# Three whole-tile additions of a two-layer graph kernel issued as accumulating transfers

## Chip, cores and metric

The kernel runs on one core of a Trainium2 chip. The metric is the device time of one execution in microseconds (us); lower is better. The engines are named as in the profile: PE is TensorE's matrix multiply and PEld its weight load, DVE is VectorE, ACT is ScalarE, POOL is GpSimd, SP is SyncE, which here only issues transfers.

## What is computed

The input is x, 16 batches of 1024 rows of 256 numbers, and an integer matrix adj of 0s and 1s, 16 x 1024 x 1024. Two graph layers follow one another, each wrapped in a residual and a layer norm:

```python
# layer 0: 4 heads of 64
h   = einsum('bnd,hde->bhne', x, W)
w   = leaky_relu(mask of edges * (e_src + e_dst));  no edge: -1e9
out = relu(softmax(w) @ h + bias) + h
out = layernorm_per_head(out) * ln_gamma + ln_beta
x   = layernorm(x + out)
# layer 1: 8 heads of 32
normed = layernorm(x) * gamma1 + beta1
out = softmax(where(adj > 0, normed @ normed.T / sqrt(32), -inf)) @ normed
x   = x + out                               # x before this line is x_in below
y   = layernorm(x) * gamma2 + beta2
mlp = gelu(y @ W1 + b1) @ W2 + b2          # 256 -> 1024 -> 256
x   = layernorm(x_in + (x + mlp))          # x_in: input of layer 1
```

The three additions that the change touches are: ln_beta to x (the "beta" of layer 0, so that one later addition brings both into the sum), the attention's output to the residual of layer 1, and b2 to that residual.

## The kernel before

All matrix work is in float32. A batch of 1024 rows is worked in two halves of 512 rows; a half lies in a tile of 128 partitions x 4 blocks x 256 numbers (128 x 1024, 512 KB). Two generators write the program: layer0 (line 955) runs over the batches and does preparation and attention of layer 0, and layer1 (line 973) follows one batch behind with attention and MLP of layer 1. A loop at the end of fast_path (from about line 1019) takes turns between them, so that PE always has the work of two batches to choose from.

The order on PE, ACT, DVE and POOL is the order in which the program is written; the loop chooses it from a model of time. The class Pace (line 90) passes every instruction on to its engine and books a start and an end for it by a table of costs; `enter` (line 151) books a transfer as landing 4 us after it may start. Work off the main line is written as chains: generators that `begin` (line 431) puts on a list with an engine and the tiles they need, and that `advance` (line 446) runs a step further once the model says that these are ready. `complete` (line 458) writes the rest of a chain at once. A step's place in an engine's queue is thus fixed by the model; on the chip an engine only waits for semaphores. SP's order is set by another scheduler, which moves a load up to where its buffer is free.

The tiles live in rings (class Ring, line 66); the ring `one` has one buffer of a name, `two` has two, and so on. xl and o0 are in `one`, x1 in `three`, layer 1's weights p in `eight`. PSUM has four buffers ps for the logits and first-layer products, two acc, two po.

The places that the change and the prediction touch:

- **Layer 0, after the attention (after0, line 638).** It runs for a pair of heads, so twice a half (hd = 1 and hd = 3), on the tile hb, called o there. DVE subtracts the mean per head, ACT squares (into oT), DVE sums (v0s), POOL takes the power -1/2 (tile r; `power`, line 347), DVE multiplies by gamma and then by r. With hd = 3 the tile xl is taken and x loaded into it by SP (line 657), DVE adds ln_beta to it (line 668), and DVE adds xl to hb (line 674). From there the norms that lead to layer 1's input (sq, nT, v) and to its residual x1 follow.
- **Layer 0's attention (attention0, line 567)** needs DVE for its weights (p<-cb,dinv,mask) and PE for acc<-v,p; preparation (prepare, line 484) puts acc<-w0e,xT on PE, small copies and `rows` on ACT, z<-acc,bias and v<-z,v on DVE.
- **Layer 1's attention (attention1, line 722).** A step: four logits matmuls on PE into the four ps, four exponentials on ACT (p<-ps), two mask products on DVE (p<-p,mask), and, three steps later, PE's products (po<-p,v, po<-p,unit, po<-v,p). PE can write the logits of the next step only when ACT has read the ps buffers. A half takes 16 steps; the tile o0 (o<-po,ranges) gathers its heads.
- **The residual of layer 1 (finish1, line 840),** once a half: DVE adds x1 to o (o<-o,x), takes statistics, writes v1s; POOL takes the power (r<-v1s); DVE adds o to x1 (x<-x,o, line 852) and computes t; ACT normalises o **in place** with four activations (o<-o,t,r; scale_shift, line 362); PE transposes o (acc or ps<-ident,o) and ACT copies it to yT. So o is read by the addition of line 852 and then overwritten by ACT.
- **The bias (add_bias2, line 861),** a chain of its own that half_done (line 986) begins, due 24 us of model time later: x1 += b2 on DVE. Here b2_r holds b2 - beta1.
- **The MLP (mlp, line 872).** PE forms ps<-yT,w_sb, ACT the Gelu (hid<-ps,b_sb), PE po<-w_sb,hid. `second` (line 889) completes the bias chain before it starts; last_norm (line 931) adds x1 to po on DVE (z<-po,x), norms it with a power on POOL and four small steps, and SP stores it.

The first half's finish1 falls in the middle of layer 1's attention, the second half's at the start of the MLP. POOL also issues the loads of adj (tile ak, line 476), which turn int32 into bfloat16 on the way.

Of the kernel before, what the change touches and what calls it, by code (L numbers as in the profile page):

```python
# [31 lines left out]
F32 = mybir.dt.float32  # L32
# [4 lines left out]
OP = mybir.AluOpType  # L37
PSUM = bass.MemoryType.PSUM

P = 128  # L40
# [49 lines left out]
class Pace:  # L90
# [60 lines left out]
    def enter(self, engine, op, args, kwargs):  # L151
        aps = [a for a in (*args, *kwargs.values()) if isinstance(a, bass.AP)]
        out, ins = aps[0].tensor.name, [a.tensor.name for a in aps[1:]]
        if op == "dma_start":
            start = max(self.now(), self.through(out))
            self.written[out] = start + self.LATENCY["sync"]
            return
        start = max(
            [self.free[engine], self.read.get(out, 0.0)] + [self.written.get(i, 0.0) for i in ins if i != out]
        )  # L160
        cost = self.cost(engine, op, aps, args[2] if len(args) > 2 else None)
        if engine == "tensor":
            if start > self.free[engine] + 1.5:
                self.slow = start + 3.0
            if start < self.slow:
                cost *= 2.0
        end = self.free[engine] = start + cost
        self.written[out] = max(self.written.get(out, 0.0), end + self.LATENCY[engine])
        if "accum_out" in kwargs:
            out = kwargs["accum_out"].tensor.name  # L170
            self.written[out] = max(self.written.get(out, 0.0), end + self.LATENCY[engine])
        for i in ins:
            self.read[i] = max(self.read.get(i, 0.0), end)
# [3 lines left out]
def fast_path(  # L177
# [24 lines left out]
    nc = Pace(tc.nc)  # L202
# [112 lines left out]
    def at_time(t):  # L315
        return lambda: t
# [141 lines left out]
    def complete(chain):  # L458

        for item in list(chains):  # L460
            if item[0] is chain:
                while item in chains:
                    run(item)


    def load_x(t, b, k, count):
        nc.sync.dma_start(t, x[b, k * P : (k + count) * P, :].rearrange("(g p) d -> p g d", p=P))
# [170 lines left out]
    def after0(b, n, hd, o):  # L638


        for first in range(hd + 1):
            complete(residuals[b, n, first])
        rowwise = [P, BPH, D]
        heads = slice((hd - PAIR + 1) * HO, (hd + 1) * HO)
        oh = o[:, :, heads].rearrange("p g (h e) -> p g h e", e=HO)
        per_head = [P, BPH, PAIR, HO]
        s = small.tile([P, BPH, PAIR], F32, name="s0")
        nc.vector.tensor_reduce(s, oh, axis=mybir.AxisListType.X, op=OP.add)
        nc.vector.scalar_tensor_tensor(
            oh, s[:, :, :, None].to_broadcast(per_head), -1.0 / HO, oh, op0=OP.mult, op1=OP.add  # L650
        )
        yield "scalar", o
        sq = two.tile([P, BPH, PAIR * HO], F32, name="oT1")
        nc.scalar.activation(sq, o[:, :, heads], AF.Square)
        if hd == H0 - 1:
            xl = one.tile(rowwise, F32, name="xl")
            load_x(xl, b, n * BPH, BPH)
        yield "vector", sq
        v = small.tile([P, BPH, PAIR], F32, name="v0s")
        nc.vector.tensor_reduce(  # L660
            v, sq.rearrange("p g (h e) -> p g h e", e=HO), axis=mybir.AxisListType.X, op=OP.add
        )
        nc.vector.tensor_scalar(v, v, 1.0 / HO, EPS_HEAD, op0=OP.mult, op1=OP.add)
        r = power(v.rearrange("p g e -> p (g e)"), BPH * PAIR, "r0").rearrange("p (g e) -> p g e", e=PAIR)
        pair = o[:, :, heads]
        nc.vector.tensor_mul(pair, pair, lng0_r[:, None, heads].to_broadcast([P, BPH, PAIR * HO]))
        if hd == H0 - 1:
            nc.vector.tensor_add(xl, xl, lnb0_r[:, None, :].to_broadcast(rowwise))
        yield "vector", r
        nc.vector.tensor_mul(oh, oh, r[:, :, :, None].to_broadcast(per_head))  # L670
        if hd < H0 - 1:
            return
        complete(norms[b, n, PAIR - 1])
        nc.vector.tensor_add(o, o, xl)
        yield "vector", o
        mv = small.tile([P, BPH, 2], F32, name="mv0")
        for g in range(BPH):
            statistics(o[:, g, :], mv[:, g, :])

        v2 = small.tile([P, 2, BPH], F32, name="v2")
        nc.vector.tensor_scalar(v2[:, 0, :], mv[:, :, 1], 1.0 + EPS, EPS * EPS, op0=OP.mult, op1=OP.add)
        r2 = power(v2[:, 0, :], BPH, "r2")
        nc.vector.tensor_scalar(v2[:, 1, :], mv[:, :, 1], EPS, None, op0=OP.add)
        r3 = power(v2[:, 1, :], BPH, "r3")
        yield "vector", r2
        t = minus_mean(mv[:, :, 0], r2, BPH)
        yield "scalar", t
        normed = one.tile(rowwise, F32, name="sq")  # L690
        scale_shift(normed, o, t, r2, BPH)
        yield "tensor", normed, side_ready
        nT = two.tile([P, DC, HALF], F32, name="nT")
        for g in range(0, BPH, GB):
            transpose_rows(nT[:, :, g * P : (g + GB) * P], normed[:, g : g + GB, :], g1_c, be1_c)
            yield "tensor", normed, side_ready
        yield "vector", normed
        v1 = two.tile([P, BPH, H1, HD + 1], F32, name="v1")
        nc.vector.memset(v1[:, :, :, HD], 1.0)
        for g in range(BPH):  # L700
            nc.vector.tensor_mul(
                v1[:, g, :, 0:HD],
                normed[:, g, :].rearrange("p (h e) -> p h e", e=HD),
                g1_r.rearrange("p (h e) -> p h e", e=HD),
            )
        handed[b, n] = [None, v1, nT]
        yield "vector", r3

        ratio = small.tile([P, BPH], F32, name="ratio")
        nc.vector.tensor_mul(ratio, v2[:, 0, :], r2)  # L710
        nc.vector.tensor_mul(ratio, ratio, r3)
        yield "vector", ratio, at_time(nc.now() + 12.0)

        x1 = three.tile(rowwise, F32, name="x1")
        for g in range(BPH):
            nc.vector.scalar_tensor_tensor(
                x1[:, g, :], normed[:, g, :], ratio[:, g : g + 1], be1_r, op0=OP.mult, op1=OP.add
            )
        handed[b, n][0] = x1
# [120 lines left out]
    def finish1(o, x1, yT, heads):  # L840


        complete(heads)
        rowwise = [P, BPH, D]
        nc.vector.tensor_add(o, o, x1)
        mv = small.tile([P, BPH, 2], F32, name="mv1")
        for g in range(BPH):
            statistics(o[:, g, :], mv[:, g, :])
        v = small.tile([P, BPH], F32, name="v1s")
        nc.vector.tensor_scalar(v, mv[:, :, 1], EPS, None, op0=OP.add)  # L850
        r = power(v, BPH, "r1")
        nc.vector.tensor_add(x1, x1, o)
        yield "vector", r
        t = minus_mean(mv[:, :, 0], r, BPH)
        yield "scalar", t
        scale_shift(o, o, t, r, BPH)
        for g in range(0, BPH, GB):
            yield "tensor", o, side_ready
            transpose_rows(yT[:, :, g * P : (g + GB) * P], o[:, g : g + GB, :])

    def add_bias2(x1):
        nc.vector.tensor_add(x1, x1, b2_r[:, None, :].to_broadcast([P, BPH, D]))
        yield from ()

    def in_range(values):
# [78 lines left out]


    handed = {}
    norms, residuals = {}, {}

    def finish_norms(b, n):
        for chain in [c for at, c in norms.items() if at[:2] == (b, n)]:  # L950
# [22 lines left out]
    def layer1():  # L973
        for b in range(B):
            place[1][:] = b, 0.0
            seen, rinv1, mask = handed.pop(b)

            def half(n):
                if (b, n) not in handed:
                    finish_norms(b, n)  # L980
                return handed[b, n]

            yT = [two.tile([P, DC, HALF], F32, name="yT") for _ in range(NH)]
            halves = {}

            def half_done(n, o, heads):
                finish_norms(b, n)
                x1 = handed[b, n][0]
                chain = finish1(o, x1, yT[n], heads)
                bias = add_bias2(x1)  # L990
                halves[n] = x1, yT[n], chain, bias
                begin(chain, "vector", done(heads), o)
                begin(bias, "vector", at_time(nc.now() + 24.0), x1)

            yield from attention1(half, mask, rinv1, half_done)
            complete(weights_of_later)
            yield from mlp(b, halves)
            in_range(seen)
# [490 lines left out]
```

## Time and profile before

| | us |
|---|---|
| three runs | 3454.31, 3445.69, 3454.04 |
| median | 3454.04 |
| span of the profiled execution, first to last instruction | 3453.7 |
| the profiled execution's own time | not listed apart from its span |
| PE busy | 3312.8 (96%) |
| DVE busy | 2981.3 (86%) |
| ACT busy | 1935.6 (56%) |
| POOL busy | 418.6 (12%) |
| mean granted clock of PE | 0.980 |

How to read the profile. A group line names the source line (L61 for all, since one helper records every instruction, so tiles tell the groups apart), the engine, the operation, out<-in by the program's tile names without their numbers, and the shape; then busy us and mean ns of one, and after the second bar the idle time of the engine just before these instructions with what ended it. A timeline line begins with the start and the length in us; in square brackets stands idle time before it. In a line of the waits the numbers are us in total, how many times, and the longest. In the table of stretches every engine has its busy time in that stretch. "issue" means that the engine waited for nothing that the profile shows. The chain of waits is followed back from the last instruction, at each step to what released it. A queue line of transfers gives packets, MB and the share of 16 transfer engines that they took; an issue line gives KB each and the median us from issue to landing. Several waits ending together are put down to the last one.

### The profile page before, as it was taken

The page shows a single profiled execution, that of the slowest core. Times are in us where ns is not written, and L with a number is a line of the kernel's source. Part 1 is how long each engine was busy: PE and PEld are TensorE (multiplying, and loading weights), DVE is VectorE, ACT ScalarE, POOL GpSimd, SP SyncE. Part 2 cuts the span into 40 slices and gives each one's busy share as a digit, 9 for nine tenths or more (in the row PEclk, how much of TensorE's full clock was granted, in tenths as well). Part 3 has the DMA queues.
Part 4 walks back from the last instruction along what each step waited for, and adds up shares of the span by engine and source line. Part 5 has one row for each costly group of instructions (what it writes and reads, how often), then busy time and mean ns, then how long its engine had stood idle before and what let it go on. Part 6 is the DMA issues. An engine that isn't in the chain of part 4 may idle for free.

```text
span 3453.7 us, 141035 instructions
## 1 busy us (share of the span) xinstructions
PE 3312.8 (96%) x64161; PEld 2252.1 (65%) x64161; DVE 2981.3 (86%) x5262; ACT 1935.6 (56%) x4192; POOL 418.6 (12%) x424
## 2 busy tenths in 40 slices
PE   5899999999999999999999999999999999999998
PEld 4558576675856758576585766757667585775846
DVE  5898898988979898898988989889898898989883
ACT  2563846547375573746637466473654737556373
POOL 1102011010110101101020110101101011010200
PEclk9899999999999999999999999999999999999999
DMA  5211202011020111202112020120201102010000
GB/s 135 51 22 40 44 27 57 15 44 40 28 59 21 42 34 34 56 19 59 22 38 46 24 57 19 41 43 26 59 15 46 38 28 62 18 44 23 23 6 15
DMA packets 95728, 131.30 MB, mean 38 GB/s; under 512 B 10385, under 2 KB 61585, under 8 KB 95121
## 3 DMA queue, kind: packets, MB, share of 16 engines
q1 hardware_dynamic: 75104, 87.58, 8.2%
q0 software_dynamic: 18432, 33.56, 6.6%
q8 instruction: 504, 8.26, 1.0%
q10 hardware_dynamic: 1584, 1.05, 0.1%
q14 instruction: 104, 0.84, 0.1%
HBM read 138.68 MB, written 17.04 MB: 45 GB/s over the span
## 4 chain that ended last, share of the span: by engine, by line
PE 72%; DVE 20%; ACT 5%; issue 2%; DMA 1%; POOL 0%; SPq 0%; POOLq 0%; ACTq 0%; DVEq 0%
PE po L61 28%; PE ps L61 24%; PE acc L61 20%; DVE p L61 15%; ACT p L61 2%; DVE o L61 1%; DVE x L61 1%; ACT sq L61 1%; DVE st L61 1%; DVE z L61 1%; ACT mask L61 1%; ACT hb L61 1%; DVE v L61 0%; ACT z L61 0%; DVE hb L61 0%
## 5 line engine op out<-in xcount | busy, mean ns | idle before, releaser
L61 ACT ACTIVATE p<-ps 128x512 f32<-128x512 f32 x2006 | 1042.2, 616 | 384.1 <-PE ps L61 341.5
L61 DVE TENSOR_TENSOR p<-p,mask 128x1024 f32<-128x1024 f32 x1024 | 1186.6, 1217 | 6.8 <-ACT p L61 6.8
L61 DVE SCALAR_TENSOR_TENSOR p<-cb,dinv,mask 128x512 f32<-128x512 f32 x1024 | 711.0, 744 | 0.1
L61 ACT ACTIVATE hid<-ps,b_sb 128x256 f32<-128x256 f32 x512 | 242.0, 473 | 795.0 <-PE ps L61 794.7
L61 PE MATMUL ps<-nT 32*128 32x512 f32 x4012 | 676.3, 655 | 0.0
L61 PEld LDWEIGHTS po<-v,p 128*32 128x32 f32 x32768 | 396.1, 110 | 333.2 <-issue 288.5
L61 PE MATMUL acc<-v,p 128*64 128x65 f32 x16384 | 562.2, 226 | 31.0 <-DVE p L61 14.3
L61 PEld LDWEIGHTS acc<-v,p 128*64 128x64 f32 x16384 | 515.2, 140 | 112.9 <-issue 59.0
L61 PE MATMUL po<-p,v 128*32 128x512 f32 x2048 | 552.9, 615 | 0.0
L61 PE MATMUL po<-p,unit 128*32 128x512 f32 x2048 | 552.7, 615 | 0.0
L61 PE MATMUL ps<-yT,w_sb 128*128 128x256 f32 x2048 | 489.8, 385 | 0.0
L61 PE MATMUL po<-w_sb,hid 128*128 128x256 f32 x2048 | 474.6, 384 | 0.0
L61 PEld LDWEIGHTS po<-w_sb,hid 128*128 128x128 f32 x2048 | 381.7, 190 | 54.5
L61 PEld LDWEIGHTS ps<-yT,w_sb 128*128 128x128 f32 x2048 | 375.5, 190 | 51.5
L61 PE MATMUL po<-v,p 128*32 128x33 f32 x32768 | 391.4, 199 | 12.4 <-issue 8.5
L61 PEld LDWEIGHTS po<-p,v 128*32 128x32 f32 x2048 | 78.5, 109 | 332.9 <-issue 174.7
L61 PEld LDWEIGHTS ps<-nT 32*128 32x128 f32 x4012 | 220.1, 186 | 98.0 <-issue 41.3
L61 POOL TENSOR_TENSOR r<-v,mhalf 128x1 f32<-128x1 f32 (+1 forms) x192 | 157.6, 831 | 705.7 <-DVE v L61 623.8
L61 DVE TENSOR_TENSOR z<-acc,bias_r 128x256 f32<-128x256 f32 x128 | 54.1, 423 | 181.7 <-ACT hb L61 181.4
L61 PE MATMUL acc<-w0e,xT 128*128 128x264 f32 x512 | 154.1, 425 | 37.2 <-DVE z L61 22.9
L61 POOL DMA_DIRECT2D ak<-in_adj_dram x128 | 69.7, 545 | 971.5 <-PE acc L61 959.0
L61 POOL TENSOR_TENSOR r<-v1s,mhalf 128x4 f32<-128x4 f32 x32 | 61.5, 1922 | 981.1 <-DVE v1s L61 981.1
(111 smaller groups left out, 2818.5 us busy)
## 6 DMA issues: line engine op xcount, KB each, us to landing
ak<-in_adj_dram POOLq DMA_DIRECT2D x128, 256.0 KB, 3.9
cb<-esr SPq DMA_DIRECT2D x64, 512.0 KB
xk<-in_x_dram SPq DMA_DIRECT2D x64, 256.0 KB
xl<-in_x_dram SPq DMA_DIRECT2D x32, 512.0 KB
out_dram<-z SPq DMA_DIRECT2D x128, 128.0 KB
w_sb<-in_L_gnn_W_dram SPq DMA_DIRECT2D x2, 1024.0 KB
esr<-rows SPq DMA_DIRECT2D x64, 4.0 KB
v<-in_L_gnn_a_src_dram SPq DMA_DIRECT2D x2, 320.0 KB
```

Of the source, the lines that this page charges most:

```text
L61: return method(*args, **kwargs)
```

## The change

Three VectorE additions, each once a half and so 32 times, become transfers that GpSimd issues with an accumulating operation (destination = destination + source).

- x1 += o (finish1) is issued behind the power of the same step.
- x1 += b2 is the chain `accumulate`, begun at the same due time as before, but for GpSimd. Its source is b2_r, broadcast over the four blocks.
- xl += ln_beta is a chain as well. xl is now taken and loaded with the half's first pair of heads (hd = 1) instead of its second; xl being in a ring of one, a tile that is still open has its chain completed first. Before xl is added to hb, `settle` makes sure that the chain has been written.
- Pace books a transfer's sources too: it may start when they are written, and they count as read until it lands, 4 us after its start.

```diff
         if op == "dma_start":
-            start = max(self.now(), self.through(out))
+            start = max([self.now(), self.through(out)] + [self.written.get(i, 0.0) for i in ins])
             self.written[out] = start + self.LATENCY["sync"]
+            for i in ins:
+                self.read[i] = max(self.read.get(i, 0.0), self.written[out])
             return
...
-        if hd == H0 - 1:
-            xl = one.tile(rowwise, F32, name="xl")
+        if hd < H0 - 1:
+            for at in list(with_x):
+                complete(norms[(*at, H0 - 1)])
+            xl = with_x[b, n] = one.tile(rowwise, F32, name="xl")
             load_x(xl, b, n * BPH, BPH)
+            begin(accumulate(xl, lnb0_r[:, None, :].to_broadcast(rowwise)), "gpsimd", xl)
...
-        if hd == H0 - 1:
-            nc.vector.tensor_add(xl, xl, lnb0_r[:, None, :].to_broadcast(rowwise))
...
         complete(norms[b, n, PAIR - 1])
+        xl = with_x.pop((b, n))
+        settle(xl.tensor.name)
         nc.vector.tensor_add(o, o, xl)
...
-        nc.vector.tensor_add(x1, x1, o)
+        nc.gpsimd.dma_start(x1, o, accum_op=OP.add)
...
-    def add_bias2(x1):
-        nc.vector.tensor_add(x1, x1, b2_r[:, None, :].to_broadcast([P, BPH, D]))
+    def accumulate(dst, src):
+        nc.gpsimd.dma_start(dst, src, accum_op=OP.add)
         yield from ()
...
-    norms, residuals = {}, {}
+    norms, residuals, with_x = {}, {}, {}
...
-                bias = add_bias2(x1)
+                bias = accumulate(x1, b2_r[:, None, :].to_broadcast([P, BPH, D]))
...
-                begin(bias, "vector", at_time(nc.now() + 24.0), x1)
+                begin(bias, "gpsimd", at_time(nc.now() + 24.0), x1)
```

## Prediction

> **What bounds the kernel now.** I read the engine totals and a table of eight batch-long stretches first.
> ```profile
> PE 3312.8 (96%) x64161; PEld 2252.1 (65%) x64161; DVE 2981.3 (86%) x5262; ACT 1935.6 (56%) x4192; POOL 418.6 (12%) x424
> ```
> ```profile
> sum 1684.00, PE 1645.27 PEld 1117.54 DVE 1485.29 ACT 966.96 POOL 208.54; mean PE 205.66 PEld 139.69 DVE 185.66 ACT 120.87 POOL 26.07
> ```
> TensorE is busy 205.7 of 210.5 us (1684/8) in a batch, 98%. VectorE has 185.7. Whatever relieves VectorE can win at most PE's idle 4.8 us a batch, 77 us in 16, and only where that idle is a wait for VectorE. The chain of waits seems to say more:
> ```profile
> PE 72%; DVE 20%; ACT 5%; issue 2%; DMA 1%; POOL 0%; SPq 0%; POOLq 0%; ACTq 0%; DVEq 0%
> ```
> Most of the 20% is "DVE p", the mask product before layer 1's products. The timeline of weight loads shows what such a step is worth:
> ```profile
> 415.14 0.11 PEld L61 LDWEIGHTS po<-p,v 128*32 128x32 f32 x1 [0.76 <-issue]
> 418.14 0.11 PEld L61 LDWEIGHTS po<-p,v 128*32 128x32 f32 x1 [0.76 <-DVE p L61]
> ```
> The gap is 0.76 us whether VectorE ended it or nothing did: it lies beside the running logits. So VectorE is just in time, not late. PE's own idle names it seldom (table of waits):
> ```profile
> PE acc L61 <- DVE z L61: 41.3, 37, 2.3
> PE acc L61 <- DVE p L61: 14.3, 9, 3.9
> ```
> **What the Trainium skill says.** "DMA: Bandwidth & Descriptors", section "SWDGE vs HWDGE vs iDMA": an accumulating DMA must come from GpSimd, whose cores write the descriptors in software. Its section "Anatomy of one DMA — SWDGE (gpsimd) path" prices one at 2.0 us plus bytes/436e3; for the 512 KB that an ak load reads that is 3.2, the trace has 3.9. "Collectives: The Full Stack", section "The bandwidth ceiling: the fold count and why AG ≠ RS ≠ AR": an add in a DMA needs two source reads and runs at about half a copy's rate (62.28/32.35). This trace shows no adding transfer. "SBUF — State Buffer", section "Who interferes with whom": a VectorE instruction with two SBUF inputs contends with a GpSimd instruction that reads SBUF. The trace agrees: the power r of v1s takes 1.91 us beside x+o, two like ones with little beside them 1.98 together.
>
> **Part 1, VectorE loses 96 adds.** Groups by shape:
> ```profile
> L61 DVE TENSOR_TENSOR xl<-xl,lnb_r 128x1024 f32<-128x1024 f32 x32 | 39.2, 1224 | 0.0
> L61 DVE TENSOR_TENSOR x<-x,b_r 128x1024 f32<-128x1024 f32 x32 | 39.0, 1218 | 0.0
> L61 DVE TENSOR_TENSOR x<-x,o 128x1024 f32<-128x1024 f32 x32 | 39.0, 1217 | 0.0
> ```
> 39.2 + 39.0 + 39.0 = 117 us off VectorE, 7.3 a batch. On the path: in the batch from 1253 us PE waits for "DVE z" twice, 1.40 us at 1390.2 and 1.63 at 1394.8. The second follows an idle VectorE (waiting for ACT hb), so no saving reaches it. The first follows the add to xl at 1381.30, after which VectorE idled 0.43 us for a power. That power ran beside the add and may end sooner without it. I give the whole 1.40: 16 × 1.4 = 22 us. Bounds 0 and 55 (both wait lines); 22 is taken.
>
> **Part 2, the length of an adding transfer.**
> ```profile
> q0 software_dynamic: 18432, 33.56, 6.6%
> ak<-in_adj_dram POOLq DMA_DIRECT2D x128, 256.0 KB, 3.9
> ```
> q0 holds only the 128 ak loads: 0.066 × 3453.7 / 128 = 1.78 us of all engines each, so 3.9 − 1.78 = 2.1 is fixed. An ak load reads 512 KB (int32) and writes 256 KB; the add reads 2 × 512 KB and writes 512 KB. By bytes read, data takes 3.56 and landing L = 5.7 us: my value. Lower end 3.9 (the second read is free). Upper end: bytes written double and the second read doubles again, 7.1 + 2.1 = 9.2.
>
> **Part 3, x1 += o: ScalarE now waits for a landing.** scale_shift overwrites o in place, so in the built order its first instruction waits for the transfer that reads o, 32 times. Behind it in ScalarE's queue stand exponentials or Gelus, and PE waits for those through four ps buffers. Both places recur in each batch.
>
> First half (within layer 1's attention), batch at 412:
> ```profile
> 411.98 2.06 ACT L61 ACTIVATE p<-ps 128x512 f32<-128x512 f32 x4 [0.48 <-PE ps L61]
> 413.93 0.40 ACT L61 ACTIVATE rows<-acc 128x256 f32<-128x256 f32 x1
> 414.98 2.06 ACT L61 ACTIVATE p<-ps 128x512 f32<-128x512 f32 x4 [0.66 <-PE ps L61]
> 416.90 2.08 ACT L61 ACTIVATE o<-o,t,r 128x256 f32<-128x256 f32 x4
> 422.54 1.14 PE L61 MATMUL ps<-nT 32*128 32x512 f32 x8
> ```
> The changed order puts scale_shift ahead of rows and the next four exponentials (the planner sees VectorE free earlier). The power ends at 412.07 and the transfer is issued there. Landing 412.07 + 5.7 = 417.8; scale_shift to 419.9, rows to 420.3, exponentials to 422.3; then PE's logits 1.07 (the shortest such group), products 1.56, layer 0's products 1.09 and logits 1.14 end at 427.2. Before, that last group ended at 422.54 + 1.14 = 423.7. Loss 3.5, that is L − 2.2.
>
> Second half (start of the MLP):
> ```profile
> 461.83 1.91 POOL L61 TENSOR_TENSOR r<-v1s,mhalf 128x4 f32<-128x4 f32 x1 [49.76 <-DVE v1s L61]
> 464.12 2.06 ACT L61 ACTIVATE o<-o,t,r 128x256 f32<-128x256 f32 x4
> 466.82 0.47 ACT L61 ACTIVATE hid<-ps,b_sb 128x256 f32<-128x256 f32 x1 [0.64 <-PE ps L61]
> 466.62 1.04 PE L61 MATMUL ps<-ident,o 128*128 128x128 f32 x8
> 467.50 1.03 PE L61 MATMUL ps<-yT,w_sb 128*128 128x256 f32 x4
> ```
> Order unchanged. With x+o off VectorE the power ends some 0.9 us sooner, at 462.85 (0 if the contention stays). Landing 468.55, scale_shift to 470.6, the Gelu to 471.1, and PE's next first-layer product, which needs its ps buffer, starts then instead of at 467.50. Loss 3.6, that is L − 2.1.
>
> Together 7.1 a batch, × 16 = 114 us. With L = 3.9: 1.7 + 1.8 = 3.5, 56 us. With L = 9.2: 7.0 + 7.1 = 14.1, 226 us.
>
> **Part 4, the other transfers, costed at nothing.** Each issue takes GpSimd about what an ak issue takes (0.55 us): 96 × 0.55 = 53 us on an engine that is 12% busy; a broadcast source, in runs of 1 KB and so in four times the pieces, up to 2.2 as an estimate. Their cover: xl += beta follows the power at 470.71, which ends at 472.7, and the next power starts at 477.15. It lands near 479, the add of xl to hb is at 498.7; the second half's is issued by about 527, used at 541.6. The load of xl stands at the same place in SP's queue and was issued long before, so GpSimd doesn't wait for it. The bias of the first half follows x1 += o at once and holds GpSimd for L; its next instruction comes 49 us later. The second half's bias is issued at 478, with the next power at 484.0. ak loads come from 535 on. If such a cover failed, the powers, and behind them ScalarE's z, would come late by 1 to 2 us each.
>
> **Sum** against the profiled span, 3453.7 us (no separate time of that execution is given; the median of the runs, 3454.04, is 0.3 above): 3453.7 + 114 − 22 = 3545.7, 2.7% slower. With the ends of L: 3488 and 3658.
>
> **Rivals.** (a) Faster: VectorE sets the pace of layer 1's attention after all, as "DVE p" in the chain and its 0 us of idle there suggest. Then all 117 us come back, and the first half's waits vanish beside VectorE's backlog; only the second half's cost, 16 × 3.6 = 58, is paid: 3453.7 − 117 + 58 = 3395 us. It decides once half of the 117 reaches PE. Against it: the equal gaps of 0.76. (b) No change: the transfer lands like an ak load (56 us lost) and PE's later waits, up to 55 us by the two lines, vanish because VectorE has caught up: 3455 us. Against: most of those waits don't follow a removed add. (c) Slower still: powers queue behind transfers. Some 8 powers a batch stand behind one; at 0.5 to 1 us each on PE, 64 to 128 us on top: 3610 to 3674 us. For: GpSimd is in order. Against: the gaps of 4 to 49 us named above. That the change doesn't do what it says can be set aside: the built order has 96 fewer VectorE and 96 more GpSimd instructions.
>
> **Chances.** Main case 0.65, (a) 0.13, (b) 0.12, (c) 0.10. About 0.3% (10 us) is what a measurement of this kernel can tell from no change. Faster 0.13, within 0.3% 0.12, slower 0.75. Range 3445 to 3650: it takes in (b), the main case and most of (c), and leaves out (a) and the far end of L; the main case alone is 3488 to 3658.
>
> **What would show it.** Right: VectorE's busy time falls by about 117 us; ScalarE's o<-o,t,r has new idle ahead of it, ended by a DMA, 3 to 5 us, 32 times; PE's idle grows by some 7 us a batch at 417 to 422 and 467 to 471 us; landings near 5.7. Wrong: landings under 3 us, ScalarE's idle not followed by PE idle, or the products' 0.76 us gaps shrinking where VectorE got faster.

## The result, and the profile after

| | before | changed |
|---|---|---|
| median of the runs, us | 3451.25 (3445.69 to 3454.31) | 3553.14 (3549.09 to 3561.37) |
| ratio, with its 95% interval | | 1.0291 (1.027 to 1.0313) |
| span of the profiled execution, us | 3453.7 | 3549.5 |
| DVE busy, us | 2981.3 | 2885.6 |
| PE busy, us | 3312.8 | 3369.0 |
| mean granted clock of PE | 0.980 | 0.969 |

The change costs 102 us. The forecast was 3546 us, 92 us more than before. The experiments show that its mechanism was right, that its waits were forecast some 46 us too long, and that it left out a cost of about the same size, the clock of PE. So the number is as close as it is partly by luck.

The engine totals of the changed kernel, and its chain of waits:

```profile
PE 3369.0 (95%) x64161; PEld 2282.9 (64%) x64161; DVE 2885.6 (81%) x5166; ACT 1937.9 (55%) x4192; POOL 524.6 (15%) x520
...
PE 75%; DVE 10%; ACT 6%; DMA 5%; issue 2%; POOL 1%; ACTq 0%; SPq 0%; POOLq 0%; DVEq 0%
```

VectorE is busy 96 us less (the three groups of 117 us are gone as forecast; the total falls by less because it counts overlapping instructions once), and in the chain its share falls from 20% to 10%. Yet PE, which does exactly the same 64161 matmuls, is busy 56 us longer. That is the first riddle. DMA has grown in the chain, from 1% to 5%, and 4% are x<-o. The table of waits says where:

```profile
ACT o L61 <- DMA x<-o: 98.0, 32, 4.5
...
POOL x L61 <- DMA x<-o: 70.4, 16, 4.8
...
PE acc L61 <- DVE z L61: 32.3, 27, 1.8
...
PE ps L61 <- ACT o L61: 18.2, 15, 1.8
...
PE acc L61 <- ACT o L61: 15.1, 15, 1.4
PE acc L61 <- DVE p L61: 13.1, 11, 1.9
PE acc L61 <- ACT rows L61: 12.2, 15, 0.8
```

ScalarE waits 32 times, 3.1 us each, for the landing of x<-o before it may overwrite o. PE has three new waits (18.2, 15.1 and 12.2 us), which add up to only 45.5 us. The waits for "DVE z" and "DVE p", all that VectorE could give back, have gone from 55.6 to 45.4. The landings are the last number in the lines of the DMA issues:

```profile
ak<-in_adj_dram POOLq DMA_DIRECT2D x128, 256.0 KB, 3.9
...
xl<-lnb_r POOLq DMA_DIRECT2D x32, 512.0 KB, 5.5
x<-o POOLq DMA_DIRECT2D x32, 512.0 KB, 4.7
x<-b_r POOLq DMA_DIRECT2D x32, 512.0 KB, 6.0
```

The first half's stall in the batch at 1280, in the timelines of POOL, ACT and PE:

```profile
1280.36 1.93 POOL L61 TENSOR_TENSOR r<-v1s,mhalf 128x4 f32<-128x4 f32 x1 [6.12 <-DVE v1s L61]
1282.26 0.90 POOL L61 DMA_DIRECT2D x<-o  x1
1287.12 1.30 POOL L61 DMA_DIRECT2D x<-b_r  x1 [3.96 <-DMA x<-o]
```
```profile
1286.91 2.08 ACT L61 ACTIVATE o<-o,t,r 128x256 f32<-128x256 f32 x4 [2.64 <-DMA x<-o]
1288.89 0.36 ACT L61 ACTIVATE rows<-acc 128x256 f32<-128x256 f32 x1
1289.15 2.03 ACT L61 ACTIVATE p<-ps 128x512 f32<-128x512 f32 x4
```
```profile
1287.56 0.93 PE L61 MATMUL acc<-ident,o 128*128 128x128 f32 x4 [0.56 <-ACT o L61]
1289.30 0.66 PE L61 MATMUL acc<-ident,o 128*128 128x128 f32 x4 [0.81 <-ACT rows L61]
1289.89 3.42 PE L61 MATMUL ps<-nT 32*128 32x512 f32 x8
...
1297.85 1.14 PE L61 MATMUL ps<-nT 32*128 32x512 f32 x8
```

The transfer is issued at 1282.26 and lands just before 1287; o, rows and the four exponentials follow one another as forecast. PE's waits of 0.56 and 0.81 us are visible. A third one is hidden: the logits group of 1289.89 takes 3.42 us where the next one takes 1.14. Its eight matmuls start one after another, from 1289.89 to 1292.25, as the exponentials free their ps buffers; matmuls overlap, so such waits inside a group count as busy. But that is not all of the riddle: the exponentials end at 1291.18, and the last two of these matmuls start only at 1291.66 and 1292.25. The table of stretches has busy time of PE, PEld, DVE, ACT, POOL, each with its number of instructions, then PE's granted clock, the DMA share and GB/s:

```profile
1284.00:1287.00 3.00, 3.00 (x82) 1.49 (x80) 3.00 (x5) 0.36 (x2) 0.00 (x0) 1.00 0.83 158
1287.00:1290.00 3.00, 1.58 (x9) 0.94 (x10) 3.00 (x6) 3.00 (x7) 1.30 (x1) 1.00 0.37 55
1290.00:1293.00 3.00, 3.00 (x8) 1.36 (x8) 3.00 (x3) 3.00 (x8) 0.00 (x0) 0.65 0.84 121
1293.00:1296.00 3.00, 3.00 (x75) 1.39 (x74) 3.00 (x5) 1.10 (x3) 0.00 (x0) 0.50 0.00 0
1296.00:1299.00 3.00, 3.00 (x48) 2.17 (x48) 1.89 (x2) 0.00 (x0) 0.00 (x0) 0.71 0.02 5
```

After the stall the clock column falls from 1.00 to 0.50. By the trace's records of the granted clock, PE has half its clock from 1290.89 to 1297.72, so it works at half speed for 6.8 us, nearly all of them *after* ScalarE has caught up at 1291.18. Added up over the whole trace by these records, the stretches at half clock that begin within 14 us of a wait for x<-o cost 46.1 us in the first halves and 6.8 in the second ones (half of each stretch's length counted as lost). In the kernel before, no such stretch lies at these places. This resolves most of the riddle: with half of PE's busy time in all half-clock stretches counted as lost, the loss is 63 us in the trace before and 102 in the changed one. These are 38 of PE's 56 us more; the rest is taken to be waits inside groups.

### The profile page after: what moved, and what is told of

The parts are those of the page before. It is cut to its first block, busy times and chain, and to the rows that moved or that the text cites. A ratio compares the mean times of both kernels' runs of the same rounds, so it can differ in the third digit from the quotient of the medians.

```text
span 3549.5 us, 141136 instructions
## 1 busy us (share of the span) xinstructions
PE 3369.0 (95%) x64161; PEld 2282.9 (64%) x64161; DVE 2885.6 (81%) x5166; ACT 1937.9 (55%) x4192; POOL 524.6 (15%) x520
## 4 chain that ended last, share of the span: by engine, by line
PE 75%; DVE 10%; ACT 6%; DMA 5%; issue 2%; POOL 1%; ACTq 0%; SPq 0%; POOLq 0%; DVEq 0%
PE po L61 31%; PE ps L61 24%; PE acc L61 20%; DMA x<-o 4%; DVE p L61 4%; DVE o L61 2%; ACT p L61 2%; ACT o L61 2%; POOL r L61 1%; DVE st L61 1%; DVE mv L61 1%; ACT mask L61 1%; ACT sq L61 0%; ACT hb L61 0%; DVE z L61 0%
## 5 line engine op out<-in xcount | busy, mean ns | idle before, releaser
L61 PE MATMUL ps<-nT 32*128 32x512 f32 x4012 | 698.5, 663 | 0.0
L61 PEld LDWEIGHTS ps<-nT 32*128 32x128 f32 x4012 | 232.6, 190 | 99.2 <-issue 44.1
L61 POOL TENSOR_TENSOR r<-v,mhalf 128x1 f32<-128x1 f32 (+1 forms) x192 | 174.5, 917 | 493.0 <-DVE v L61 447.8
L61 POOL TENSOR_TENSOR r<-v0s,mhalf 128x8 f32<-128x8 f32 x64 | 129.4, 2021 | 551.5 <-DVE v0s L61 551.5
```

Of the source, the lines that this page charges most:

```text
L61: return method(*args, **kwargs)
```

## The experiments

Every ratio is to the kernel before on the same chip; its medians there were 3440.18 us (runs 1 to 4), 3442.81 (5, 6, 7, 9) and 3435.97 (8, 10, 11, 12). Differences in us below are differences of ratios times 3440. Run 12 is the changed kernel measured again. The ranges in us expected for runs 1 to 4 were set from the 3451 us first measured before; the kernel before was 11 us faster on their chip, so the ratios are what to compare.

**Which transfer is it? Run 1: only x1 += o goes back to VectorE.**

```diff
-        nc.gpsimd.dma_start(x1, o, accum_op=OP.add)
+        nc.vector.tensor_add(x1, x1, o)
```


> Change undone in one part: x1 += o is again a VectorE addition; the bias and beta additions stay transfers (64 of 96). Theory (the whole loss is ScalarE's wait for the landing of x<-o): no such wait is left, 3451 us as before, within 10 us; VectorE is 78 us less busy and PE gets at most 22 us of it. Rival (GpSimd's queue and the traffic of the other two transfers delay powers): about two thirds of the loss stays, some 3515 us. Rival (VectorE's relief is worth its busy time): 3451 - 78 = 3373 us.

Measured: 3425.02 us, ratio 0.9953 (0.9934 to 0.9972). The two other additions are still transfers, and the loss is gone; the kernel is even 16 us faster than before. (Expected was the time before, within 10 us.)

**Run 2: only x1 += o is a transfer** (the kernel before, with the booking of sources in Pace).

```diff
-        nc.vector.tensor_add(x1, x1, o)
+        nc.gpsimd.dma_start(x1, o, accum_op=OP.add)
```


> One part of the change alone: only x1 += o is a transfer; the bias and beta additions are on VectorE as before. Theory (ScalarE's wait): the whole loss, 3545 to 3555 us, ScalarE idle some 98 us before o<-o,t,r. Rival (GpSimd's queue and the other two transfers): a third of the loss, about 3485 us. Rival (relief is worth something): slower than with all three by what 78 us of VectorE are worth, up to 3630 us.

Measured: 3562.53 us, 1.0357 (1.0337 to 1.0378), with ScalarE's wait as in the changed kernel:

```profile
ACT o L61 <- DMA x<-o: 97.7, 31, 4.8
```

Runs 1 and 2 put the whole loss on this one transfer. Run 2 lies above the expected 3545 to 3555 us: 23 us above the changed kernel's first ratio, but 3 above that of run 12, so it doesn't tell what the relief by the two other transfers is worth. In both runs something else goes with the transfer: in the first halves the planner moves scale_shift ahead of rows and four exponentials where x1 += o is a transfer, and behind them where it isn't. Run 3 separates the two.

**Is it the transfer or the wait for it? Run 3: ScalarE writes into another tile,** the buffer of sq, and so needn't wait. All 96 transfers stay, and ScalarE, VectorE and GpSimd do everything in the order of the changed kernel.

```diff
-        scale_shift(o, o, t, r, BPH)
+        on = one.tile(rowwise, F32, name="sq")
+        scale_shift(on, o, t, r, BPH)
...
-            transpose_rows(yT[:, :, g * P : (g + GB) * P], o[:, g : g + GB, :])
+            transpose_rows(yT[:, :, g * P : (g + GB) * P], on[:, g : g + GB, :])
```


> All three transfers stay, but ScalarE writes the normalised o to another tile (sq, then free) instead of over o, so it doesn't wait for the transfer that reads o; every order as in the changed kernel. Theory (ScalarE's wait): the loss vanishes, 3440 to 3455 us, no idle of ScalarE ended by x<-o. Rival (traffic, powers behind GpSimd's transfers): still over 3500 us. Rival (VectorE's relief is worth its 117 us once the wait is gone): 3330 to 3400 us.

Measured: 3426.89 us, 0.996 (0.9948 to 0.9973), mean clock 0.985. The group of scale_shift has no wait left:

```profile
L61 ACT ACTIVATE sq<-o,t,r 128x256 f32<-128x256 f32 x128 | 66.3, 601 | 0.1
```

**Run 4: the wait is planned around.** In place as in the changed kernel, but scale_shift is placed 11 us of model time behind the transfer.

```diff
+        landed = at_time(nc.now() + 11.0)
         yield "vector", r
         t = minus_mean(mv[:, :, 0], r, BPH)
-        yield "scalar", t
+        yield "scalar", t, landed
```


> All three transfers and the write over o stay, but the planner is told that o is free only 11 us of its time after the issue, so scale_shift stands one to two exponential groups later in ScalarE's queue; the wait stays in the program, the transfer has landed by then. Theory (it is the place of the wait, not the transfer): 3440 to 3465 us, ScalarE's idle before o<-o,t,r under 20 us. Rival (traffic or powers): over 3500 us.

Measured: 3430.77 us, 0.9974 (0.9959 to 0.999). ScalarE's wait for x<-o is down to one of 0.9 us. Runs 3 and 4 remove the wait in two different ways and have the same effect: it is the wait, not the moving of bytes, GpSimd's queue, the powers or, by run 3, the order.

**More of it. Run 5: the transfer is sent twice** (o is added twice). The second is issued when the first has landed, and lands 9.8 us after the first was issued.

```diff
         nc.gpsimd.dma_start(x1, o, accum_op=OP.add)
+        nc.nc.gpsimd.dma_start(x1, o, accum_op=OP.add)
```


> Dose up: the changed kernel, but x1 += o is sent twice, one transfer behind the other into the same tile (so o is added twice to the residual); every order is that of the changed kernel. The second can only be issued when the first has landed, 4.8 us later, so ScalarE's o<-o,t,r waits about 4.8 us more, 32 times. Theory (from the slack of about 2 us on, every us of landing reaches the end): 32 x 4.8 = 154 us on top of the changed kernel's 1.029 times before, a ratio of 1.07 to 1.08, or a little above if TensorE's clock suffers more. Rival (what costs is that PE stalls at all, by a fixed loss of clock after each stall, not how long): 1.03 to 1.045.

Measured: 3722.66 us, 1.0813 (1.0788 to 1.0837).

```profile
L61 ACT ACTIVATE o<-o,t,r 128x256 f32<-128x256 f32 x128 | 66.4, 589 | 257.4 <-DMA x<-o 249.6 <-DVE p L61 7.8
```

5.0 us more landing, 32 times, are 160 us; the time grew by 160 us (from the changed kernel's 1.0349 in run 12) to 180 us (from 1.0291). The rival of a fixed cost for each stall, whatever its length, falls. That every us of landing reaches the end as a wait is not shown, though the first sum looks like it: half of PE's busy time in all half-clock stretches is 148 us here, 102 in the changed kernel's first trace and 115 in run 12's. So 33 to 46 us of the growth are the clock, and the waits themselves account for some 120 us of the profiled spans' growth, about three quarters of the longer landing.

**Less of it. Run 10: the transfer in two pieces of 256 KB,** so that the first two activations wait for the first piece alone.

```diff
-        nc.gpsimd.dma_start(x1, o, accum_op=OP.add)
+        nc.enter("gpsimd", "dma_start", (x1, o), {})
+        for g in range(0, BPH, GB):
+            nc.nc.gpsimd.dma_start(x1[:, g : g + GB, :], o[:, g : g + GB, :], accum_op=OP.add)
```


> The changed kernel with x1 += o sent as two transfers of two blocks each (256 KB), in the same place and order; ScalarE's first two activations can start when the first piece has landed. Theory (the loss is the landing beyond about 2 us): with 2.1 us fixed and the rest of 4.8 in proportion to the bytes, a piece lands after about 3.5 us and the second is issued 0.9 us later and lands by 4.8 to 5.3; the wait is 1.3 us shorter, 32 x 1.3 = 42 us less than the changed kernel, and some halved clock less: 1.005 to 1.018 times before. Rival (two transfers at once share the engines, both land near 5 us, or the wait is for the whole tile): 1.027 to 1.035.

Measured: 3515.87 us, 1.0223 (1.0199 to 1.0247). The ratio lies between the two ranges. Against the changed kernel in the same group (1.0349) the gain is 43 us; the range had started from 1.029. That this is close to the 42 us worked out is a coincidence. The first piece lands after 3.4 us, as estimated, but the second 5.2 us after the first was issued, later than the one large transfer (4.8), and the last two activations wait for it; its issue alone takes 1.2 us. Idle time ahead of scale_shift falls only from 98.0 in the first profile (99.0 in run 12) to 80.1, 0.6 us a transfer instead of 1.3. More of the gain is the clock: the loss to half clock, counted as for run 5, is 89 us here against 115 in run 12. The group of scale_shift:

```profile
L61 ACT ACTIVATE o<-o,t,r 128x256 f32<-128x256 f32 x128 | 69.9, 593 | 80.1 <-DMA x<-o 69.7 <-DVE p L61 10.2
```

**Which half? Run 9: another tile in the first half only. Run 11: in the second half only.** (finish1 is given n; the diff is run 9's, run 11 has n == 1 in it.)

```diff
-        scale_shift(o, o, t, r, BPH)
+        on = one.tile(rowwise, F32, name="sq") if n == 0 else o
+        scale_shift(on, o, t, r, BPH)
```


> The changed kernel, but in the first half of each batch ScalarE normalises o into another tile (the buffer of sq), so that it waits for the landing only in the second half. Theory (both halves lose about the same: landing 4.8 less about 2.1 us each, and a spell of half clock after each): half of the loss stays, 1.010 to 1.016 times before. Rival (the first half carries it, since exponentials and with them layer 1's logits stand behind it): 0.998 to 1.005. Rival (the second half carries it): 1.02 to 1.03.

> The counterpart of the run with the first half freed: ScalarE normalises o into another tile in the second half of each batch only, and waits for the landing in the first. Theory (the first half's wait costs about 75 us, some 42 of it the wait and some 35 the halved clock behind it; the two halves add up): 1.016 to 1.022 times before, mean clock 0.968 to 0.974. Rival (the halves don't add: with one wait a batch fewer the other one is hidden): 1.005 to 1.012.

Measured: with the first half freed 3469.22 us, 1.0073 (1.005 to 1.0096), mean clock 0.982; with the second half freed 3496.87 us, 1.0178 (1.0157 to 1.0198), clock 0.977. Against run 3 (0.996) the second half's wait costs 0.0113, 39 us, and the first half's 0.0218, 75 us. Their sum, 114 us, gives 1.0291, the ratio first measured; run 12 stands 20 us higher. So the halves add up, within these 20 us; the ratios come from more than one chip. Run 9 fell between its ranges: the halves are not equal. The difference is mostly the clock by the traces' records, though run 11's mean of it was above the expected 0.974. In run 11 the half-clock stretches behind the first halves' waits cost 35.8 us, in run 9 those behind the second halves' 10.2.

**Is the clock a cost of its own? Run 8: PE gets dummy work in the stall,** 31 transposes a batch into the buffer of the real transposes of o. In the first half 5 of the identity go ahead of the first group (before = 5) and 8 repeats of the real ones follow each of the two groups (again = 2); in the second half 10 of the identity go ahead of the first group. ScalarE's wait stays.

```diff
         pt = side_bank([P, DC, GB, P])
+        for _ in range(before):
+            nc.nc.tensor.transpose(pt[:, 0, 0, :], ident, ident)
         for g in range(GB):
             for c in range(DC):
                 nc.tensor.transpose(pt[:, c, g, :], src[:, g, c * P : (c + 1) * P], ident)
+        for i in range(again * GB * DC):
+            g, c = divmod(i % (GB * DC), DC)
+            nc.nc.tensor.transpose(pt[:, c, g, :], src[:, g, c * P : (c + 1) * P], ident)
```


> The changed kernel with extra work for PE where it waits for o: in the first half 5 transposes of the identity ahead of the transposes of o and 8 repeats behind each of the two groups, in the second half 10 transposes of the identity ahead, all written into the buffer that the real transposes then fill; every order is that of the changed kernel. ScalarE's wait for the landing stays whole, and PE has 31 transposes a batch more to do, some 3.5 us at 0.11 us each. Theory (half of the first half's loss is PE's clock, halved for 3.4 to 6.8 us because PE stood idle in pieces of 0.5 to 2 us): the halved stretches behind this stall go, 43 us of lost clock by the trace of the changed kernel, and some 20 to 40 us come back: 1.018 to 1.024 times before, mean clock 0.975 to 0.985. Rival (the halving has another cause, and the time is that of the waits): 1.028 to 1.040, mean clock near 0.969.

> The changed kernel itself once more, to stand on the same chip beside the run with PE's stall filled. Both theories: 1.027 to 1.033 times before, mean clock near 0.969.

Measured: the changed kernel again 3556.16 us, 1.0349 (1.0328 to 1.037), clock 0.965; with the stall filled 3512.28 us, 1.0226 (1.0207 to 1.0244), clock 0.984. PE has 496 matmuls more to do and the kernel is 44 us faster. ScalarE waits as long as ever (98.5 us). The timelines of ScalarE and PE in the first half, and the stretches that follow:

```profile
1272.80 2.08 ACT L61 ACTIVATE o<-o,t,r 128x256 f32<-128x256 f32 x4 [3.36 <-DMA x<-o]
```
```profile
1272.10 0.77 PE L395 MATMUL acc<-ident 128*128 128x128 f32 x5
1273.45 0.93 PE L61 MATMUL acc<-ident,o 128*128 128x128 f32 x4 [0.59 <-ACT o L61]
1274.22 1.04 PE L401 MATMUL acc<-ident,o 128*128 128x128 f32 x8
1275.19 0.65 PE L61 MATMUL acc<-ident,o 128*128 128x128 f32 x4
1275.69 1.04 PE L401 MATMUL acc<-ident,o 128*128 128x128 f32 x8
1276.65 1.59 PE L61 MATMUL ps<-nT 32*128 32x512 f32 x8
...
1280.82 1.14 PE L61 MATMUL ps<-nT 32*128 32x512 f32 x8
```
```profile
1272.00:1275.00 3.00, 2.35 (x35) 1.84 (x22) 3.00 (x6) 2.21 (x5) 1.30 (x1) 1.00 0.05 10
1275.00:1278.00 3.00, 3.00 (x23) 1.90 (x21) 3.00 (x3) 3.00 (x8) 0.00 (x0) 1.00 1.17 170
1278.00:1281.00 3.00, 3.00 (x109) 2.12 (x112) 3.00 (x5) 1.99 (x5) 0.00 (x0) 1.00 0.03 7
1281.00:1284.00 3.00, 3.00 (x85) 1.50 (x85) 2.95 (x3) 2.03 (x4) 0.00 (x0) 1.00 0.02 5
```

The clock column stays at 1.00. From the start of scale_shift to the end of the second logits group behind it pass 9.2 us here (1272.80 to 1281.96) and 12.1 in the changed kernel (1286.91 to 1298.99). Behind the waits for x<-o the half-clock stretches cost 3.4 us in this trace and 63 in run 12's. So the rival, that the lost time is that of the waits alone, falls. The 91 us that remain above run 3 would then be the waits, and dummy work that reaches beyond them; no run separates these two.

**What is the relief worth, and do the transfers cost anything by themselves? Run 7: the kernel before in its order, without the three additions** (beta, the attention in the residual and b2 left out). **Run 6: the changed kernel in its order, with none of the transfers sent** (the same left out). In both the model of time still books them; the first two lines are run 7's, the others run 6's, and the two other additions are treated alike.

```diff
-        nc.vector.tensor_add(x1, x1, o)
+        nc.enter("vector", "tensor_add", (x1, x1, o), {})
-        nc.gpsimd.dma_start(x1, o, accum_op=OP.add)
+        nc.enter("gpsimd", "dma_start", (x1, o), {})
```


> The kernel before, its order kept by booking the three additions in the model of time, and none of them written (beta, the attention in the residual and b2 are left out of the result). This is the relief of VectorE by itself, 117 us of its busy time, in the old order. Theory (as in the prediction: PE waits for VectorE after a removed addition about 1.4 us a batch): 22 us less, 0.992 to 0.996 times before. Rival (VectorE sets the pace in layer 1's attention): 60 to 117 us less, 0.966 to 0.983. Rival (nothing of it is on the path): 0.999 to 1.001.

> The changed kernel with its order and none of the 96 transfers sent (beta, the attention in the residual and b2 are left out of the result), so neither VectorE nor a transfer does these additions. Theory (the transfers cost nothing by themselves; only ScalarE's wait for one of them did): the same as the run in which ScalarE writes to another tile, 0.996 times before, within 0.003. Rival (GpSimd's queue, its issue time or the moved bytes cost something even there): 0.98 to 0.99.

Measured: run 7 3431.4 us, 0.9964 (0.9952 to 0.9976); run 6 3417.55 us, 0.9923 (0.9906 to 0.9941). Taking 104 us of work from VectorE (2981.3 to 2877.1 us) is worth 12 us, less than the 22 expected. The expectation of run 6 is missed by a little: it is 0.0037 or 13 us below run 3. Since the changed kernel's own ratio differed by 0.006 between two groups, 13 us is no proof that the transfers cost something; they cost at most about that.

Run 7 also tells why the relief is small. VectorE in layer 0's after0, the kernel before first:

```profile
1381.30 1.22 DVE L61 TENSOR_TENSOR xl<-xl,lnb_r 128x1024 f32<-128x1024 f32 x1
1382.95 0.69 DVE L61 TENSOR_TENSOR hb<-hb,r 128x512 f32<-128x512 f32 x1 [0.43 <-POOL r L61]
```
The same place in run 7, without the addition of beta:
```profile
1374.48 0.69 DVE L61 TENSOR_TENSOR hb<-hb,lng_r 128x512 f32<-128x512 f32 x1
1376.74 0.69 DVE L61 TENSOR_TENSOR hb<-hb,r 128x512 f32<-128x512 f32 x1 [1.57 <-POOL r L61]
```
And PE a little later in run 7:
```profile
1385.41 1.74 PE L61 MATMUL acc<-w0e,xT 128*128 128x264 f32 x4 [1.40 <-DVE z L61]
```

The addition of beta had been done while VectorE had to wait for a power anyway. Without it VectorE waits 1.57 us instead of 0.43, and PE still waits its 1.40 us for "DVE z". The power itself, before and in run 7:

```profile
1380.88 2.04 POOL L61 TENSOR_TENSOR r<-v0s,mhalf 128x8 f32<-128x8 f32 x1 [2.78 <-DVE v0s L61]
```
```profile
1374.67 2.04 POOL L61 TENSOR_TENSOR r<-v0s,mhalf 128x8 f32<-128x8 f32 x1 [2.78 <-DVE v0s L61]
```

## Why the prediction came out right, step by step

**What bounds the kernel: right.** PE bounds it, and VectorE is just in time. Run 7 shows it: 104 us off VectorE give 12. Rival (a), VectorE as the pace, is refuted. The gaps ahead of the products didn't shrink either: the weight loads of po wait for "DVE p" 287 times, 177.3 us before and 177.5 in the changed kernel. In the chain, VectorE's share fell by half with hardly any time won: an engine that is just in time looks like a cause there.

**Part 1, the relief, 22 us: the step failed.** I credited the whole wait of 1.40 us at 1390.2 to the removed addition of beta, on the ground that the power beside it "may end sooner without it". The power takes 2.04 us with the addition and without it. The wait of 1.40 us is still there in run 7. The 12 us of run 7 (and 14 of run 3) come from elsewhere: in run 7 PE's waits for "DVE z" fall from 41.3 to 34.5 us; where the rest lies stays open.

**Part 2, the landing, 5.7 us: 4.8.** The fixed 2.1 us were right; the term by bytes was too large. In run 2 the queue holds the ak loads and these transfers alone:

```profile
q0 software_dynamic: 23040, 50.34, 8.8%
x<-o POOLq DMA_DIRECT2D x32, 512.0 KB, 4.8
```

They took 8.8% of 3558.5 us, 313 us. Less 128 times 1.78 for the ak loads, 85 us are left, 2.67 us for each of 32. 2.1 + 2.67 = 4.77, the measured median. (The median hides that the landings of run 2 take 5.1 us in the first halves and 4.6 in the second; why is not shown.) So reading twice the bytes cost 1.5 times an ak load's time, not twice. Part 2 alone made the forecast 0.9 us x 32 = 30 us too high. "Collectives: The Full Stack" of the Trainium skill, section "The bandwidth ceiling: the fold count and why AG ≠ RS ≠ AR", on which I had leaned, has a factor near two to a plain copy, for collectives; no plain copy of this size was run here, and the ak load, which converts its numbers, is not one.

**Part 3, the wait of ScalarE: right in place, order and count,** 32 waits ended by the DMA, 3.1 us each on the mean. The growth of PE's idle, forecast as 7 us a batch, is only 2.5 (span less busy time, 140.9 us before and 180.5 after, over 16 batches); the rest of the waits lies inside groups that count as busy. With L = 4.8 the prediction's two rules give 2.6 us a batch in the first half and 2.7 in the second, 42 + 43 us. Measured were 75 and 39.
- First half: taking the 35.8 us of lost clock off the 75 leaves 39 us for the wait, close to 42. The clock is what the prediction lacked altogether. It counted PE's groups after the stall at full speed: from the landing to the end of that last logits group it has 9.4 us (417.8 to 427.2). Run 8, at full clock, takes 9.2; the changed kernel takes 12.1.
- Second half: the power ended sooner, as said (1.03 us instead of 1.91), and 39 less 10.2 of clock leaves 29 for the wait. So this half's slack, the part of the landing that costs nothing, is some 0.7 to 0.9 us larger than I read (with that half's own landing of 4.6, or with 4.8); where it lies is not shown.

**Part 4, the other transfers at nothing: right** within 13 us (runs 3 and 6). Issues of a broadcast source hold GpSimd for 1.3 us, one of x<-o for 0.9 instead of the 0.55 forecast, and no power came late enough to matter. Rival (c) is refuted.

**The sum.** Forecast +114 − 22 = +92. Measured: about +68 for the waits, +46 for the clock behind them, −14 for the relief (run 3) are +100, of a measured 102. Only the clock's 46 is a size of its own (in the changed kernel's own trace it is 53); the 68 are what it leaves of the two halves' 114. Rival (b), no change, falls with it: the landing was shorter than 5.7, but PE's waits for VectorE didn't vanish. The 114 us of Part 3 agree with the runs' 114 by accident: a landing and a slack mis-sized by some 45 us in total, and 46 us of clock that were left out.

The clock could have been seen. In the kernel before, the half-clock stretches cost 72 us counted the same way, 17 of them in the first 205 us and the others mostly one a batch, behind places like the two waits for "DVE z" near 1390 to 1396, and Pace itself books matmuls at double cost for 3 us after PE has stood idle for 1.5. "TensorE: Matmul & The Clock Gate" of the Trainium skill, section "What's actually happening", tells of two states, half and full, decided over windows of 3.4 us. The records here agree: 0.5 or 1.0, at half clock for 3.41 us or multiples of it (but for the last stretch of a trace). Its table under "Why this matters for your kernels" asks only for gaps under about 3 us; here two pieces of 0.56 and 0.81 us, with a logits group behind them that waited for exponentials, were followed by half clock, and not when run 8 filled them in part. The measurement decides.

## What to carry to other kernels

Before an addition is handed to a transfer, look for who writes its source next: here VectorE gave the tile back after 1.2 us and the transfer after 4.8, and an in-place step behind it inherits the difference, with everything queued behind that. Where PE bounds the kernel, price a stall of PE with the half-speed stretch that follows; here that was 46 us beside 68 us of waits. Relief of an engine that is just in time is worth what its waits show, and only if nothing else ends at the same moment: measure it by leaving the work out in an unchanged order, as run 7 did.

Of the kernels here, those that keep ScalarE from waiting (runs 1, 3, 4) beat the kernel before by 0.3 to 0.5%; run 1 (two of three additions as transfers, 0.9953) and run 3 (all three, with another tile, 0.996) are not apart by their intervals.

## What the runs showed of the hardware

- PE at half clock: behind a stall in which PE was busy 1.58 of 3 us the clock was halved for 6.8 us; behind one with 2.35 us (run 8) it was not. These are two places and no threshold.
- An adding transfer of 512 KB within SBUF lands after 4.8 us, one of 256 KB after 3.4. With a source broadcast over four blocks 512 KB take 5.5 us (xl<-lnb_r) and 5.5 to 6.4 (x<-b_r; medians of the runs). Issuing holds GpSimd for 0.9 us, with the broadcast source 1.3.
- The power of 128x4 takes 1.93 us in the first half, where VectorE works on p<-p,mask beside it, and 1.03 in the second half of the changed kernel, where x+o no longer runs beside it.
